# One expert table for both batches: layer 1's mixture of experts in 39 tiles instead of twice 23

## The chip, the core and the metric

The kernel runs on one core of a Trainium2 chip. Its time is measured on the device, in microseconds (us) for one execution; the kernel before takes 1811.49 us, the median of 19 runs that lie between 1807.17 and 1817.41 us. The engines are named as the profile names them: PE multiplies matrices (PEld loads its weights), DVE and ACT work element by element, POOL (GpSimd) issues the gathers and some element-wise work, and SP issues the plain transfers.

## What is computed

A model of four layers works on two batches of 1024 tokens with 128 features, all in float32. Each layer normalizes its input, computes an attention part `s` and a feed-forward part `g` from the same normalized input, and adds the product:

```python
xn = _layernorm(x, axis=-1)
s = _L1_attn_ref(xn, ...)
g = _silu(_L1_ffn_ref(xn, ...))
x = x + s * g
```

The feed-forward part of layer 1 is a mixture of experts. Eight experts, each a 128-to-512 product, a GELU and a 512-to-128 product; every token goes to the two of highest probability, whose results are added with these probabilities as weights:

```python
probs = jax.nn.softmax(jnp.einsum('bsd,ed->bse', x, Wr), axis=-1)
topv, topi = jax.lax.top_k(probs, K)                      # K = 2
h = jax.nn.gelu(jnp.einsum('bsd,dh->bsh', x, w1) + bb1, approximate=False)
y = jnp.einsum('bsh,hd->bsd', h, w2) + bb2
acc = acc + ce[..., None] * y                             # over the 8 experts
```

Nothing in it joins the two batches.

## The kernel before

The program is first recorded and then issued. Every call such as `C.mm(...)` or `nc.vector.tensor_add(...)` only notes an operation; products of one kind that follow each other are collected in one unit (`Record.note`, `Record.product`). A unit carries what it depends on. `Record.order` then reads a fixed order of all units from a packed string, `ORDER`, which was searched offline with a planner's costs, together with the place in memory of each buffer (`PLACES`). `Record.issue` emits the units in this order, so each engine's queue is fixed when the kernel is built, and every instruction of the profile carries the one line of `issue`, L584. The parts of the program are told apart by the names of their tiles.

The order interleaves freely: while one batch is in layer 1, the other may be in layer 0 or 2, as far as data allow. An instruction waits in its engine's queue until its inputs and its buffer are there, and everything behind it waits too.

Layer 1 has two parts.

- `l1_attn`, once for each batch: 64 steps of four `sim` products (scores, 32 rows deep), four exponentials on ACT (`e<-sim,own`, 128x512) and four `av` products that add up the weighted values. A finished sum is copied out by DVE (`asb<-av`).
- `l1_ffn`, once for each batch. It writes the normalized tokens to a table in memory (`xd`), takes the router's probabilities, ranks the experts of each token and counts the tokens of each expert (`rank`, `sel`, `before`, `place`). Each expert's tokens get whole tiles of 128 rows. For 2048 choices (1024 tokens, two experts each) and 8 experts there are at most (2048 + 8 * 127) // 128 = 23 tiles. 32 products (`fill`, 46 columns wide) put into a table which token stands in which row and with which weight. Then, for each tile, POOL gathers its 128 tokens (`xg<-xd,token`, 64 KB) and the weights of its expert (`we<-in_experts,expert`, 526 KB). Four `up` products, a bias on DVE, a GELU on ACT, and four `down` products follow; up to four tiles share one transposition, one scaling by the weight (`y<-down,weight`), and one write to a second table (`yd`). Last, POOL gathers the two results of each token back, 16 gathers of 128 rows each (`y<-yd,slots`), and DVE adds them (`g<-g,y`).

The layer's end (`step`) takes the SiLU of `g`, multiplies it by `s` and adds it to `x`; then the normalization of layer 2 (`ln_m`, `ln_sq`, `ln_v`, `ln_r`, `xn`) and the transposition `tr<-const,xn` of that batch can start. In layer 2, `l2_ffn` compares all tokens' router weights on DVE (`j<-wall,wtok`), and `l2_attn` runs the products `pk`, `pq`, `pg`.

The expert weights use the pool of 35 large buffers (`half`), the gathered tokens and the hidden values the pool of 21 buffers of 128x512 (`t512`), which also holds the exponentials of the attention. A gather is released when the buffer's former user has finished.

Of the kernel before, what the change touches and what calls it, by code (L numbers as in the profile page):

```python
# [19 lines left out]
I32 = mybir.dt.int32  # L20
# [5 lines left out]
P = 128  # L26
# [173 lines left out]
def _constants():  # L200
# [33 lines left out]
        "token": p + P * c[:, :8],  # L234
# [35 lines left out]
def pack_inputs(inputs):  # L270
# [38 lines left out]
    "c-nP&2VfLc_x+ytW@cx1Q%EI*gc^Dk5S1!H1O*F4P*4=%6G0IavCy(K!4Cv!is*;ZMN|}2iZmhg-g^rz1k#huwwd>TZ)SJ1!QX#LHd9`?@7{CIJ@0||XiL"  # L309
    "%ZXCXdr8|Xg0gHMv+rLh+fU7Uny6yB>{RM(AzF4Tr5;gZdL`$_y&2eej$InQhvxv=y0F()V*<Fx8o-5+bw_!)AeFops@KEDB;J|~q1XJc`_<}T|i#v~{^@"  # L310
    "C37INe=)Cgy^-Ec~3=2Os|63HwHJ)0vcQO2VSe&Zq;u{a4B}*-8yq`>!aivH-MQRSy+L6PVV>x6Q;iVH?E*MZV*1^NZzf;dOd}y*W&NXS+FJ~<@jqAStVx"
    "8*q0=ydJqG2ZGwkCyE~L$Z_XVMA+738mJTK!#Shqi5>KPM@HHzw#pkM2l=O{w(x*~J!{`1SGiCAEbe-zd^&4L7@o_eiE_?)sL|pSQYz2G+q4;I(8#wT6<&"
    "mGee(hc9{%3RZEse&%SNY5j>W~_^opQKp^4(<M*^R)hRAg5XV_&Lkm~yiko><|pPj%opks85|GtJI5<S&dboavB<SmdElhJBw@_QG~_!q%4j1w(u;@E~E="
    "3!U+^&7D(uFMoJ(pw(-AurcXrEbG_xfBlZoD?=x@?fw=XxHjOqZ})Uo{VLv@FEL6M4OM}3_`5c_C-aVkWkG$vWA8fYWYI5uc=V6q5m*avW1xM|;>B-%--@"
    "<!+upzr9i`6P{d1=ueC$3n8*n38xe@ZJ1S}ZQ=D4HD>BoVmCpW0XpKbi?*Tnm~`T&$X_SH>3QPtv427jA*?s9Ftpyu_W#%EKCip!K|327%yL)-mrFBHVO@"
    "+2uct$5Ua;IV_{F*}C$bMbbQoRkRzSGBECQ_3l-cC)b7wPtrxhr}w$OQC5?-a2sg-*K<-A=ps($l*Bi=B3hzcKGMXKdpZM6Nr;RN3@e1ko_{213iCxiLa>"
    "luUOGbfB!6qhhjrt(W@W^yMc%_9AEm5;-e)OS{CceB-c~WE5|A`ti$hF0kr^F{_%ohjQn8|uIDL^TKLEhJIBHZbrudN38^CPKvqQDsIR>y7%nRIlG?bIa("
    "&P*eKM~}o_QZM8uG#1IR*}HR29w@pX9ByKB{Dk%Y+<aJgQW9I|Wh2#Zf5Aw?;(b7HarCstBNh%XMgGo4gBc_Eo#trVD-;v?YB<SD!@5cRf}6xG58r2)_%H"
    "c=XAC{Y8){9G=KBt0v`wLgKd)|6Bekjv|hnh*EH@5<a%^k^PXicR_SfH1~`ztIpk_UR~N#QkI|i=2DWAbnj(J^3p%=k<`0Le44I`?y(xam~0iLR=iFsXA`"
    "Ud_cu6Sblc4BSOJ`G{*R)4iT6)o2wW-_Z(rMYQx2_^m;4k~ClL0OIq#-|o=J;oZ-Da<u%<uycYRgiREA|<6@{R2lAcpJ`$yBv52Y(nOYllnlo6tl0wrp8V"  # L320
    "Jx(|9Vm46U4b#)bneT!{UTKlUz{shJjt%%oD7|2soXpDkB+OJmE!&It6O$y0<09@zs~eH;fH+d+P?g+KcO&Icm<TP0#xBHdI7(e5k{GfKh+DBNd8UF163p"
    "WyD~fFYb|T6arX)*`>l{zA@?|EV@@-|=gGKJj#=}M>^1DV=Yti?W4fq4=B8npr2Tm3L)W<ZJ}V<A`S1sBKt7_~gnacX5{e}~0%Ysc+R0XWQH)*|NeI*3k%"
    "YMwnN^bXf~OA<O31y$K?Jj@hvU5rv9)FY^ry7yIkdFKdz&ul9;sAulp#^lq1VsUFQEy&n1(jHWg=<1#O$2TQKm#u=7K|8|J84xRxb}pKRgpt5T9R(F^}lU"
    "!G2ZDo*Uzi6JD=}gH}*C2nDwT_esprR6M4gh!ZX=KrD|_4Al$r0f!Q!7YTwQyn<+dNT?BmD!NV58S%$cM)IPIDCdSIINDlb`&&^a@%Zpi5b9DmFIVA&dqd"
    "TKMju@!@GDlgX6L=ixY;)M9UU>(%6Pr_HM9MuF9%X8tA4^{MtF71eSR2{4#<bH&?usE<-zTL{`2HqGNbweyisjFVq82HCF)<@(fO(ijbq0?_T~G&uYr|v*"
    "2lVp8RG_Z_FwU8_OvxGM?XVXM-_kFJm)n$rOx4ncMQc0e8K~1C#=o>eV;#46W5;n_-~A!{lyrUW9H(^wzu(R6>7z~DtysJ98lEJo)amzI-d7>513VDv{zF"
    "Y(>(Htf_CpXC@WLq@}o=Ux;S#Ca90(A%qYS3OyaA;otqQy;huNJ55X7FlxVCdp5(>*$V=;ASjUlRfVIokGFmWT1JzR(y(b-4>N9eS<B$VpF_Cm_eKD0(tg"
    "&CMts!FW`}wgY_Sxef|FZ{2?w(S0IvVTOM`HSTnsU1}R@FeYJEX7@N>y1Z?YWUq$=&o^+kBjDM4O&^<`0~9MM|YAq4iJKz2>$N9xlGhq|3>YM($P5N^pzn"
    "O>*N6$Y<+riTRbx{-wRhLQMHu;~Zn<5SE~N9QH!Kwn+M&zVJAs91f|s^9L^f^aq|TE-3E2K=MTMgjabAefM|5hSWQa@iUe9iX`1Zcee$Jjlqd{iE&p_jzL"
    "C<)opwElaZNw(Mn<myLR2mfs_X>EttKSMDPZsk+c#D^fER6e07epLaW{5mvvTI(r`bDv%Z6y7{$HKvr4<28u#{?G#pzr|Lmf19s%JLUjEG-jN=^&lL_vBR"  # L330
    "P-xhcN2~+4CC1a_b9abIDfqvCXUJMtX*lKe>{EcEDm^wNDt~!6pgcq&BK#D5xDDto#&#WGl@Hq2sZgRDh_E^pQ_ArY+BL~>GH`7kJQ5a@$0&6?z|p<USGM"
    "s*-4DqjIPM_->j95{D>p1Qfz0Ay@u6jaqR?}wTt+v!TD$Vw?278Lq_$jT?Q)8wd{7f`4RhC+GA|Y<vu+Ip~j6R*MXDGaN>JT{iE9gsjXaO(`$cj!;%FtE8"
    "p7C*WEFbzipm^xhXGvm5Sv*ebsZ+lar2LcrvNjrEsP7(-2YAYpr>K{buX=%8QRe+0%!jbny2HMYJ@5^W}M@qU8PWvSK;y7y9&#Z!GS27uc%lqwf7^O@Dn;"
    "PI8yO(PiuE{wpL8=fuVMzQK|<gU}SC3Stu@3Zj>PXWe|QHqahTrbfvab_&uuuG`YF{Uxj_cnRBkVqH6BdpeG!@9Icr4Z<;9I@<C+61a$9R8Rgxr!BBKA@?"
    "bA3}|*Tn-NPj@4YVgd%$0vN)qo={DC&Nxr#+xjo8z-+G5SeS7WxsJ$N2_+a}7my>8MWUVSz<MoY|hV#|z-^ZSrCa8?X<HEGxwf7^MnXt>W?b%?yb&g`9i@"
    "UHCNft^xZ|F7Oz)?`mRT=|c{f?a1@@j>11I%e)XQ8MV~+)V7zXQ9c=o{tSbyeTfPacq7K*L_)IR{9N(>5Ero9C>3YUi1ztT64=@R&8CcbwC3?PE>JyTxxR"
    "sR9Dc5i%pkw;t~ekZ&tf`j;wge*6sK7ozffUGrBgIuvWW)s+cz0UJyaA&KiSz%ckR8Ay?hQ&eh|}dl8zxS^r}mRlFX#x$RP(Wh>vsoJ(~}F8+CiA$HhyE4"
    "auT`TdnzM=|2yV+V&9jR59d!~!~J`Pp}{W7tmz-oo}c)JjFdQCxX|H?Pe@(x}Blv5Itzx`qEa2F^(+nK~b+)BP`?#}|D+Z{227H(0-Hd?-PuNPC<MU!5wM"
    "?RQ#9w`^>~*(fxseblZsaV?pkT`feiEzXCl7g7t_XS(CBqe)yPa=MZ4S`CuDWZYT%2K3$7E$;={yTaWS*!G_lj68a5=exV(v(rlub%haEQwcZk9Iw-PA4x"
    "rLE$uqv)9szJmLe)0myzB4K%F%84)VHvRqf8uEr${sNe3chha>LJjE1q5y5gn8x5p6H;<Nks67Tq@WhXazZso=2uKu-jG`Zgm17E|V4T{o`sl7O}I`zE#J"  # L340
    "sZ5_LCq7(CR!@x!d)2O;_#?%-*P}&+4_>+-dSzdd&3n^PK<SmZ+xXMqi&7K(Hj<AYBdFzIy`OkxarxtUjO+I8=me^2yeoJfibnm(SGiApZa4<XXmJ6k36L"
    "p&868M_{iL`{eF$UvSzS9(f$cR{$ZPYlcGC3YNvMZMZHvMC2qw!hF<+4>7A>-;zzmoYJI?uT}R(0*2b5=ScLccku|gN0lxlV4oV~P#%n3}VmJd4S?kgU89"
    "5}fwDR-6m6C|Dc(;@cDT};?Go3S8+qNS<s>aCl^qdnDz|n|l<LTJx<3EM<(-~8y7U8{hc{_U!CXNo>-?Pqg%P56h6wPaVq)(9%g{!D7eY<-(6i%=?oVw-c"
    "EY+3y+m2H^($^%8B=Wu4yABp)yNjMkJ?`uK#fO=2-PIx^%HrB>wiTfAZJ-8LzP=2NVulZ>ufEa-7#h*b5D-f^eCMGx#1Al{)-_A*QJAzIZTkI4dDYJ&?h*"
    "RhOf1V^TWvS~m~({FK<h)tAK`7Uq#cg!{XhTP#~xLdl1yOs+P**U{d$mX_7R8ULBf7)BX3@xyU1R$qiSy)`F2=y>?JqF97((D;yP^4ZXEFb3kk!%k3Ebgr"
    ">ob!T$_|WUpfT|BNj@D@h%QilE-4Npj8Cfi3TLshCG(v6t27iH`?61l^mT18eOJ1y8Nj-yq-#zi!tvTcrfx0kgmTWKd#Bu+}kD0(ffLCOx2Ucx2oM5iuEn"
    "uec4`WTej}SR~^<8U$1qlh8rX3A9ZNXAwT{eQ{+%e;tn^DD6qxIIQ7hyZl_!-OVpGU>N^yp+aKMcH$TzX=BN7ACMRtzPU2DAQqSs<$wYG9sCV1XOHB3a)v"
    "uO4c={}z`N`*BH3d0O^|n_b>9wYli03=8AKLEpVf%j~uarbTmW%6DUo&9UjN~&H6W6|#tJJun_|+8yt~T<VlKY>fO%9z^>YZsyPeZMF+0_Rdo6=;i;jVu@"
    "97=VN@83M(J40y?E4!pt*K~(=5e*rk7v}rfDD9hhmonQ(bk4|{S@XDly}kzjs~M-x9y3Fh9mtbExW0qt&3kcVde8m`@px}k`hY%AWvbR3xCSrAyrxoEHFe"
    "fBz$Z5T^39evWo7>(aecfI^Q?(?l*{#AS;`z)sRug4ujWy%4xb}2C}CD@d57~I_oR$jaKO%Y<9&Chp7h#I&RAK7M{WCP(}us{pP7H7!%slvoleKm+@yl&="  # L350
    "6^hQ;=C^PK6@S0-y5(R{o&i#V{6w9U3P2U>_kcN;reTc>Waya<8_XlNzRt^*o)WF^jn(ZwjS&l|HzSFXe&D4mo9&F-q~@lA2l!WR7vbW|NF*SM%u4H3!J}"
    "1s-!;n<iD+<IQR(XBM&t^(&7|Tp4rju$}w53eY@5zBr7=3idnBb-gx&#zL5o5ad0aN&iUGK%~1yIv$j^ZciY^0-zb`b-+FA_+kw{kwyxa$vli+h45XJ1+>"
    "hwIhgMb910Cz8@LkKKcHJg`j-US4i54hHy_0sa9@&DlD}T4>u|WlRtwd}~O*xXw93I{3wd#NHZI+hlSj~DOsqvi?>~VF6EsE4UpsH$N<-*uo{4cHI@U85a"
    "N+RhVwLZ5>jUtcZr+({7R9hUL1I;4)6~ek@Z_^7R)H0P)+Y?(7TAZf0*}>1S{<Gt2J1Q(wlA+s+m3G!mtxmSnk2F67IfmX#(vq-c@McPDD9m=Gu?qF{{6z"
    "<~r}lYhSws`ZUPn`}c0g_C(Gjr~PdN5by%pq=NFP0jC(!H0QTS_kkKoei*+XzSRe}b4$<4;gdz?NUIe>C$($ozVId>6NrD${dCfNN?WTKtE4R7IEUi^*vr"
    "z0AdZUz^O&x4#k*Ryio>4wyLruZ=%#$Yz!-%4H4w2aG1zSVI>(n2?xj&U9A$lYHWQ;oO~Lli7%;;3_?sYhP@XnyRoo0>jIzT5N%+snX(6^AzeGksjDZIm-"
    "@4@s_4c#o00nH|`kPm$SvYKMA^IQ)vI^8L!YSW|uY3lzP6=X;T7b{>l@_*ll*^`$4SJSZwol+M>;t(SbXsok>dk@$i*m&Q=yj(qy>#);o^l^lg6H)rb?<@"
    "H^xIP{oHP~2AcbDUharEeBDPk%<oUe4+~Gc~&P*PmQR?z;H*qL!*2RL?r{`S0FWeY|wT6E$H_wIZkO)Blc{J7MnVA88ljr^XRf1Kcl}`*w8EM%EqgcRJVX"
    "e*CEExO556KzW@?w^LknWz7BwgFe`lx*@juc)eIXb>`rkzfCM7Rj*HJ(PiemSvZ{wYwi5_(TKkjV;vC{6A;wHRj+Lx{)71+&AhPWY`wze;<VwZZ5T#|)%f"
    "(%=GwKcVP;RHts8M0m#}@(3Jm;mA>T(_X!KX&=Wlj@;n(@MaI=07KG3lK>C0+iSm!O@R-KW4o_sLAxa+eUdzVIRLz|Wh@(?%jOSs&86CjQL40Oce|12ycY"  # L360
    "}_JR7F(K^sCuF(?hZeUlU;v*cN8D2S+;|#<~N4K<t<qICf!SCe>ktyfp?b-S>XF%;k!IKOBF5c&aC{;fKTsKB|pAM*y?LvtU5LI6b@!-iT5Sl4b**W!QC<"
    "PVv4~_hH6vvzQ7}#gxRc*zU12T+RR0)<#FcCOeB@_P&{}(?2({xht}YPcj>}IybO-+`}h&G+|OlP{_=U3NE$|9zUi~KzX3kkICs>FT8CO6imTm8FiP>U76"
# [808 lines left out]
def l1_attn(C, w, xnT, b, out):  # L1171
# [157 lines left out]
    wT = C.arr("wT")  # L1329
    C.to_channels(wT, wt)  # L1330
    out["s"] = C.arr("s")
    C.project(out["s"], wT, w["wp"], w["bp"])


def l1_ffn(C, w, xn, xnT, b, out):

    nc = C.nc  # L1340
    E = 8
# [992 lines left out]
```

## Time and profile before

| what | value |
|---|---|
| median of 19 runs | 1811.49 us (1807.17 to 1817.41) |
| profiled execution, its own time | 1815.68 us |
| its span, first to last instruction | 1814.0 us |
| granted PE clock, mean | 0.958 |
| PE busy | 1649.6 us, 91% |
| DVE busy | 1206.6 us, 67% |
| ACT busy | 996.4 us, 55% |
| POOL busy | 552.3 us, 30% |
| gathers on POOL in layer 1 | 46 `we`, 46 `xg`, 32 `y` |

The profiled execution lies 4.19 us above the median, and its span 1.68 us below its own time. Busy time counts instructions that run, not waits; a group's `x` counts instructions, and one product in float32 is two matrix instructions.

### The profile page before, as it was taken

The numbers are of one execution on the slowest core, as the hardware profiler recorded it, in microseconds if no ns is written. First come the engines' busy times: TensorE is split into PE (matmuls) and PEld (weight loads), VectorE is DVE, ScalarE is ACT, GpSimd is POOL, SyncE is SP. The second block draws the span as 40 slices with busy tenths as digits, with TensorE's granted clock in tenths as the row PEclk, the third lists the DMA queues.
The fourth block names the chain that finished last, engine by engine and source line by source line (L and its number), as shares of the span: only waits on it lengthen the run. The fifth ranks groups of instructions, "written<-read, shape, count | busy, mean of one in ns | idle before, by whom it ended". The sixth has DMA issues, their size and how long they took to land.

```text
span 1814.0 us, 35482 instructions
## 1 busy us (share of the span) xinstructions
PE 1649.6 (91%) x14112; PEld 903.5 (50%) x14112; DVE 1206.6 (67%) x2371; ACT 996.4 (55%) x1775; POOL 552.3 (30%) x732
## 2 busy tenths in 40 slices
PE   7999998889699969699999999989999999999996
PEld 3464556543233823136746547743435665443374
DVE  5874895572211504333589999767988997967865
ACT  3322432249588559596465556566565565665632
POOL 1010012040511232411120165263723662873211
PEclk9998998889999979799999999999999999999998
DMA  3200010010411330313303023421003333101031
GB/s 113 32 14 2 2 34 14 2 59 24 140 38 20 118 103 20 102 17 108 116 22 102 26 67 91 137 75 61 19 5 100 98 87 90 38 28 49 24 99 45
DMA packets 96054, 106.23 MB, mean 59 GB/s; under 512 B 50224, under 2 KB 62512, under 8 KB 95760
## 3 DMA queue, kind: packets, MB, share of 16 engines
q1 hardware_dynamic: 86608, 74.11, 14.3%
q0 software_dynamic: 9280, 29.86, 5.5%
q8 instruction: 111, 1.82, 0.4%
q14 instruction: 55, 0.45, 0.1%
HBM read 87.24 MB, written 8.29 MB: 53 GB/s over the span
## 4 chain that ended last, share of the span: by engine, by line
PE 27%; DVE 18%; issue 6%; DMA 3%; ACT 3%; POOL 2%; SPq 1%; another core or an unknown queue 0%; DVEq 0%; ACTq 0%; POOLq 0%
PE sim L584 6%; DVE e L584 5%; PE num L584 4%; PE wo L584 2%; PE tr L584 2%; PE down L584 2%; DMA zb<-zd 2%; DVE qf L584 1%; DVE u L584 1%; SPq L584 1%; PE up L584 1%; PE g L584 1%; ACT e L584 1%; PE q L584 1%; PE qk L584 1%
## 5 line engine op out<-in xcount | busy, mean ns | idle before, releaser
L584 ACT ACTIVATE e<-sim,own 128x512 f32<-128x512 f32 x512 | 305.2, 704 | 90.6 <-remote 43.1
L584 ACT ACTIVATE e<-sim 128x512 f32<-128x512 f32 (+3 forms) x384 | 165.1, 499 | 94.7 <-DVE e L584 40.5
L584 PE MATMUL sim<-qT,k 32*128 32x512 f32 x1024 | 170.6, 682 | 43.4 <-DVE g L584 13.0
L584 DVE TENSOR_TENSOR e<-e 128x512 f32<-128x512 f32 (+3 forms) x320 | 171.3, 570 | 54.0 <-PE num L584 32.3
L584 PE MATMUL num<-e,v 128*64 128x64 f32 (+4 forms) x1280 | 166.7, 387 | 0.6 <-POOL e L584 0.4
L584 POOL TENSOR_SCALAR_AFFINE_SELECT e<-e 128x128 f32<-128x128 f32 x256 | 111.4, 466 | 152.6 <-ACT e L584 138.1
L584 PE MATMUL sim<-q,kT 64*128 64x512 f32 (+3 forms) x768 | 146.4, 510 | 7.1 <-ACT e L584 4.1
L584 PE MATMUL av<-e,va 128*32 128x512 f32 x1024 | 141.0, 641 | 6.2 <-ACT e L584 6.2
L584 PEld LDWEIGHTS sim<-qT,k 32*128 32x128 f32 x1024 | 53.2, 196 | 146.2 <-ACT e L584 86.1
L584 PEld LDWEIGHTS num<-e,v 128*64 128x64 f32 x1280 | 79.5, 138 | 86.3 <-issue 55.8
L584 POOL TENSOR_TENSOR sq<-qk,tab 128x256 f32<-128x256 f32 x128 | 100.7, 807 | 60.3 <-DVE ss L584 33.0
L584 PE MATMUL ph<-h,w_f 128*128 128x512 f32 x256 | 115.3, 601 | 1.1 <-DVE nn L584 0.7
L584 POOL DMA_INDIRECT we<-in_experts,expert x46 | 46.0, 999 | 205.9 <-DVE row L584 69.3
L584 PEld LDWEIGHTS sim<-q,kT 64*128 64x128 f32 x768 | 61.5, 185 | 88.2 <-ACT e L584 61.2
L584 DVE COPY asb<-av 128x512 f32<-128x512 f32 x16 | 11.1, 691 | 121.2 <-PE av L584 64.8
L584 POOL DMA_INDIRECT xg<-xd,token x46 | 45.0, 979 | 149.8 <-ACT e L584 85.6
L584 POOL TENSOR_TENSOR u<-u,sq 128x512 f32<-128x512 f32 x64 | 85.4, 1344 | 2.2
L584 ACT ACT_TABLE_LOAD x44 | 56.5, 1283 | 40.9 <-DVE h L584 7.8
L584 DVE SCALAR_TENSOR_TENSOR conv<-vT,w_a,conv 128x1024 f32<-128x1024 f32 x60 | 76.7, 1281 | 1.2
L584 PEld LDWEIGHTS ph<-h,w_f 128*128 128x128 f32 x256 | 47.9, 192 | 58.4 <-issue 54.3
L584 PEld LDWEIGHTS av<-e,va 128*32 128x32 f32 x1024 | 24.7, 112 | 95.9 <-issue 72.9
L584 ACT ACTIVATE e<-e 128x512 f32<-128x512 f32 x96 | 56.7, 626 | 27.7 <-DVE e L584 25.7
(545 smaller groups left out, 3424.9 us busy)
## 6 DMA issues: line engine op xcount, KB each, us to landing
zb<-zd SPq DMA_DIRECT2D x192, 128.0 KB
rb<-rd SPq DMA_DIRECT2D x64, 128.0 KB
w<-v SPq DMA_DIRECT2D x60, 128.0 KB
tab<-in_rotary SPq DMA_DIRECT2D x8, 512.0 KB
yd<-y SPq DMA_DIRECT2D x10, 256.0 KB
w_f<-in_f SPq DMA_DIRECT2D x4, 512.0 KB
w_l<-in_l SPq DMA_DIRECT2D x4, 512.0 KB
w_f<-in_f SPq DMA_DIRECT2D x4, 448.0 KB
```

The source lines that it names most:

```text
L584: tc.keep_in_program_order(f(*map(real, args), **{k: real(v) for k, v in kw.items()}))
```

## The change

`l1_ffn` is called once, after both batches' `l1_attn`, with the inputs of both. Both batches' tokens stand in one table `xd` of 2048 rows. The router, the ranking and the places are still made for each batch, with the second batch counting on from the first (`before`); the tiles are shared: (4096 + 8 * 127) // 128 = 39. The tables `rows`, `put` and `eq` are made for one batch and one of the two choices at a time, and the 32 `fill` products all add into one bank, now 78 columns wide. The results of both batches lie in one table `yd`, from which each batch gathers its own 32 pieces in two halves as before. The `step` of both batches comes after the call.

Products with at most 64 columns and a full 128x128 weight are collected in units of at most four, not 32. `ORDER` and `PLACES` are new: the whole program's order, all four layers, was searched anew.

```diff
-        "token": p + P * c[:, :8],
+        "token": p + P * c[:, :16],
...
-    def note(self, cost, op, args, kw, lag=SEEN, table=0, part=None):
+    def note(self, cost, op, args, kw, lag=SEEN, table=0, part=None, most=32):
...
-        if not (PE in cost and u and u.part == part and (u.batch, u.stage) == (self.batch, self.stage) and len(u.ops) < 32):
+        if not (PE in cost and u and u.part == part and (u.batch, u.stage) == (self.batch, self.stage) and len(u.ops) < most):
...
-        u = self.note({PE: 0.0}, op, args, kw, part=(tall, wide))
+        u = self.note({PE: 0.0}, op, args, kw, part=(tall, wide), most=4 if n <= 64 and tall * wide == P * P else 32)
...
-def l1_ffn(C, w, xn, xnT, b, out):
+def l1_ffn(C, w, xns, xnTs, outs):
...
-    E = 8
-    NTILE = (2 * L + E * (P - 1)) // P
+    E, NK = 8, 2
+    NTILE = (NK * NB * L + E * (P - 1)) // P
...
-    xd = C.memory("xd", [L, P])
-    nc.sync.dma_start(out=xd.rearrange("(t p) d -> p t d", p=P), in_=tiles(xn))
...
+    xd = C.memory("xd", [NB * L, P])
+    ranks, probs, sels, combs, befores = [], [], [], [], []
+    for b, (xn, xnT) in enumerate(zip(xns, xnTs)):
+        C.record.batch = b
+        nc.sync.dma_start(out=xd[b * L : (b + 1) * L].rearrange("(t p) d -> p t d", p=P), in_=tiles(xn))
...
+        before = C.t512("before")[:, : (TB + 1) * E].rearrange("p (t e) -> p t e", e=E)
+        if b:
+            nc.vector.tensor_copy(before[:, 0], befores[b - 1][:, TB])
+        else:
+            nc.gpsimd.memset(before[:, 0], 0.0)
...
+            for a in range(TB):
+                C.mm(
+                    pf[:, : 2 * NTILE], rows[:, cols(a)], put[:, a].rearrange("p s j -> p (s j)"),
+                    start=b == k == a == 0, stop=b == NB - 1 and k == NK - 1 and a == TB - 1,
+                )
...
+    for b in range(NB):
+        C.record.batch = b
+        acc, cT = C.arr("g"), C.arr("cT")
...
+        for k in range(NK):
+            y = C.arr(f"y{k}")
+            for t in range(TB):
+                gather(y[:, cols(t)], yd, slots[b][:, k * TB + t : k * TB + t + 1])
+            nc.vector.tensor_add(acc, acc, y)
+        outs[b]["g"] = acc
...
         for layer in range(4):
+            made = []
             for b in range(NB):
...
                     stage(l1_attn, weights("l1"), v[1], b, r)
-                    stage(l1_ffn, weights("l1"), *v, b, r)
+                    made.append((*v, r))
+                    continue
...
                 step(xb, r)
+            if made:
+                xns, xnTs, rs = zip(*made)
+                stage(l1_ffn, weights("l1"), xns, xnTs, rs)
+                for b in range(NB):
+                    C.record.batch = b
+                    step(x[b], rs[b])
```

In the new queues, as built, POOL has 39 `we`, 39 `xg` and 32 `y` gathers. Twelve `we` stand ahead of the first `xg`, and the rest of the 78 follow mixed; the `y` gathers of batch 0 come after the last `xg` and `we`. On PE, the last 44 `down` products (11 tiles) are followed by 32 `sim`, 36 `av` and 8 transposition products of batch 1's attention, and then by the eight transpositions `tr<-const,xn` with which batch 0 enters layer 2. Before, batch 0's `y` gathers and its `tr<-const,xn` stood among batch 1's attention, ahead of batch 1's expert tiles.

## The prediction

> **What bounds the kernel now.** I read the busy shares and the forty slices first, then the waits, then the windows and the timeline around the dips.
>
> ```profile
> PE 1649.6 (91%) x14112; PEld 903.5 (50%) x14112; DVE 1206.6 (67%) x2371; ACT 996.4 (55%) x1775; POOL 552.3 (30%) x732
> PE   7999998889699969699999999989999999999996
> DVE  5874895572211504333589999767988997967865
> PEclk9998998889999979799999999999999999999998
> ```
>
> PE is the bound: it stands still for 164.4 us of 1814.0 (1814.0 less 1649.6). The dips to 6 (slices of 45.35 us, from 454, 635 and 726 us) lie in layer 1, batch 1's attention, where DVE is nearly idle. The clock dips there too. So what the change does in layer 1 is worth PE time removed plus holes removed, less holes made. The waits name somebody who is not to blame:
>
> ```profile
> POOL y L584 <- DMA yd<-y: 45.9, 1, 45.9
> DVE asb L584 <- remote: 56.3, 2, 30.1
> DVE g L584 <- remote: 24.4, 1, 24.4
> ACT e L584 <- remote: 43.1, 10, 9.6
> ```
>
> The columns are total wait, times and longest. "Remote" is no engine of this core. The timeline shows what runs then: POOL issuing gathers back to back, one each 1.25 us (0.95 and 0.30 between), and PE standing.
>
> ```profile
> 667.98 0.95 POOL L584 DMA_INDIRECT y<-yd,slots  x1 [0.31 <-issue]
> 669.23 0.95 POOL L584 DMA_INDIRECT we<-in_experts,expert  x1 [0.30 <-issue]
> ...
> 643.78 1.14 PE L584 MATMUL sim<-qT,k 32*128 32x512 f32 x8
> 674.38 2.09 PE L584 MATMUL sim<-qT,k 32*128 32x512 f32 x8 [13.01 <-DVE g L584]
> ```
>
> The PE's hole of 13.01 us ends when the train of gathers does, and the eight matrix instructions behind it take 2.09 us against 1.14 ahead. Every such train can be priced as the PE's idle time in its window, the width less the busy time:
>
> ```profile
> core 0: us, PE busy (x) PEld busy (x) DVE busy (x) ACT busy (x) POOL busy (x), PEclk, DMA share, GB/s
> 465.00:503.00 38.00, 22.61 (x144) 6.02 (x136) 3.98 (x14) 17.88 (x30) 24.00 (x27) 0.83 0.54 177
> 590.00:618.00 28.00, 28.00 (x248) 25.64 (x247) 21.33 (x50) 16.63 (x26) 10.79 (x10) 1.00 0.41 124
> 646.00:675.00 29.00, 14.44 (x89) 5.47 (x91) 2.75 (x4) 11.25 (x19) 18.14 (x19) 0.69 0.39 118
> 730.00:761.00 31.00, 17.18 (x104) 3.95 (x100) 4.52 (x15) 14.16 (x25) 19.91 (x22) 0.76 0.48 149
> 866.00:1045.00 179.00, 169.28 (x916) 107.07 (x915) 156.47 (x308) 98.61 (x156) 29.30 (x31) 1.00 0.20 63
> ```
>
> Three long trains (27 gathers: 12 `we`, 15 `xg`; 19: batch 0's 16 `y`, 3 `we`; 21: 14 `xg`, 7 `we`) cost 15.4 + 14.6 + 13.8 = 43.8 us, 0.65 per gather. Four short ones (windows from 529, 571, 702 and 810 us, some 22 gathers) cost 1.45 + 2.87 + 1.75 + 3.26 = 9.3 us, 0.42 each. Batch 1's `y` train, among layer 2's products (895 to 921 us), costs 3.3. Spaced `we` gathers alone (590 to 618 us) cost nothing. Together 56.4 us.
>
> **The change part by part.** *A, PE work removed.* 46 tiles become 39. A tile is four `up` and four `down` products of two instructions each, and the chain of waits prices them:
>
> ```profile
> 848.12 11.61 PE up L584 x104
> 859.73 7.15 PE down L584 x64
> ```
>
> That is 0.112 us an instruction, 0.223 a product, 1.79 a tile: 7 x 1.79 = 12.5. Seven transpositions of `xg` at 0.15 (the transpositions of `asb` take 6.1 us for 40) are 1.0. The 32 `fill` products widen from 46 to 78 columns; they take 0.116 us an instruction at 46 (7.4 us for 64), products of 128 columns 0.112, so the width costs nothing. A = -13.5. The tiles' other work is priced at nothing: DVE has room beside PE (0 to 5 tenths in the slices from 408 to 861 us), and ACT's share of a tile is short.
>
> *B, the gather trains.* In the new POOL queue seven `we` and seven `xg` are gone. I grouped the rest by the PE work that frees their buffers: twelve `we` come early and spaced (nothing); 18 and then 23 (25 `xg`, 16 `we`) fall into the attention; some 25 among the expert products; batch 0's `y` train moves out of the attention (its price stands under C); batch 1's stays among layer 2's products. At the long trains' 0.65 the first 41 cost 26.7; at the short ones' 0.42 the 25 cost 10.5; batch 1's `y` 3.3. Sum 40.5, so B = -15.9. Ends: everything in attention at 0.42 and the 25 free, 20.5 (B = -35.9); all 66 at 0.65, 46.2 (B = -10.2). I keep 0.65 in the attention because three trains agree on it.
>
> The Trainium skill ("Trainium Architecture — The Big Picture", section "What this means for kernel authors") says that the engines' lanes into SBUF and the DMA ports can't contend. By it a train costs PE nothing of itself, B would be 0 and the sum +23. The 13.01 us hole, under a POOL that does nothing but issue gathers, speaks against taking it so far.
>
> *C, a new hole between layers 1 and 2.* This is the part that speaks against the change. Before, batch 0's way into layer 2 (last `yd` store, sixteen `y` gathers, sum, SiLU, normalization, transposition) lies under batch 1's attention, and batch 1's under batch 0's layer 2:
>
> ```profile
> 889.58 1.16 DVE L584 TENSOR_TENSOR y<-down,weight 128x384 f32<-128x384 f32 x2
> 895.23 0.94 POOL L584 DMA_INDIRECT y<-yd,slots  x1 [45.91 <-DMA yd<-y]
> 917.02 0.94 POOL L584 DMA_INDIRECT y<-yd,slots  x1 [0.30 <-issue]
> 919.57 1.23 DVE L584 TENSOR_TENSOR g<-g,y 128x1024 f32<-128x1024 f32 x1 [2.61 <-DMA y<-yd,slots]
> 942.81 1.04 PE L584 MATMUL tr<-const,xn 128*128 128x128 f32 x8
> ```
>
> After, batch 0 needs all 39 tiles before its first `y` gather, and batch 1's experts are done by then. By the rows: 5.65 us from the last `y` product to the first gather, 15 x 1.25 = 18.8 to the last, 2.55 to the sum, 1.23 for it, 14.45 from SiLU (696.85) to transposition (711.30), as batch 0 did it, and one load of ACT's function table, 1.28. Together 44; batch 1's row, from 889.58 to 942.81, took 53.2 among layer 2's work. What covers it is what the new PE queue puts between the last `down` and `tr<-const,xn`: 32 `sim` and 36 `av` products, eight steps of attention. A step is four exponentials on ACT, one behind the other 2.42 us, a little more than its PE work. 8 x 2.42 = 19.4. So C = +24.6 (44 - 19.4); ends +23 (the same with the table load hidden) and +34 (53.2 - 19.4).
>
> The skill's page "TensorE: Matmul & The Clock Gate" (section "What's actually happening") says that PE falls to half clock once it has idled some 3.4 us, and needs as long a stretch of work to recover; by it this hole costs an estimated 1.7 us more. The row of 2.09 against 1.14 us shows the half clock after a long hole.
>
> *D, batch 0's comparisons on DVE.* Layer 2's `j<-wall,wtok` (mean 0.747 us, 46 in all, and 16 of 0.35) is some 20 us a batch. Batch 0's ran from 727 us, under batch 1's attention; now it stands at the start of layer 2, where DVE is busy 156.5 of 179 us. Room is 22.5, less its bad placing; between 0 and 20 I take +8 (no gain: DVE stood idle where they were).
>
> *F, late weights.* After, the expert products of all 39 tiles run nearly in one piece, and the last 14 tiles need their 526 KB each within it. At the 149 to 177 GB/s of the train windows a tile's weights take 3.0 to 3.5 us against 1.79 of PE, but the queue runs ahead by the buffers. Weights can't be earlier than needed to any gain; 0 to 10, I take +4.
>
> *The units of four and the new order elsewhere.* Layers 0, 2 and 3 keep their sequence nearly as it was on all queues; nothing taken, 10 us either way. ACT loads as many tables as before.
>
> Sum: -13.5 - 15.9 + 24.6 + 8 + 4 = +7.2. The profiled execution's span of 1814.0 becomes 1821.2; its own time, 1.68 above, 1822.9; that execution lay 4.19 above the median, so the median becomes 1818.7.
>
> **The rivals.** *Faster.* Trains that stand among expert products cost nothing (28.00 busy of 28.00 from 590 to 618 us, though only `we`), those in the attention 0.535, the mean of both prices, and the weights arrive in time: 41 x 0.535 + 3.3 = 25.2, B = -31.2, F = 0, sum -12.1, time 1799.4. Against it stand the expert window from 810 us, which lost 3.26 of 10, and three trains at 0.65.
>
> *Much slower (the other end of my own side).* The way into layer 2 takes batch 1's 53.2 us, the comparisons lie bare, the weights are late: -13.5 - 10.2 + 34 + 20 + 10 = +40.3, time 1851.8. For it: DVE's nines in layer 2. Against: in the hole POOL and DVE have little else, whereas batch 1's train shared both with layer 2.
>
> *No net change, or the change is undone elsewhere.* Gains and losses cancel, B near -23, or B as taken with D at 0 (sum -0.8); or the new order loses or wins some 7 us in layers 0 and 3. Time 1811.5.
>
> Faster becomes the outcome once the trains cost under 33 us in all: with F at nothing the sum is +19 and B.
>
> **How the numbers follow.** A measurement of this kernel can tell 0.2%, 3.6 us. My forecast has 0.40 (slower, 1815 to 1835), the faster rival 0.37, the cancelling one 0.11, the much slower one 0.12. Faster 0.37, same 0.11, slower 0.52. The range must take in the faster rival with some of B's lower end and most of the way to the much slower one: 1790 to 1846; outside it lie half of that rival and a little of B's low end. The predicted time is the forecast's, 1818.7.
>
> **What would show it.** In the profile after: PE's matrix instructions fewer by 119 (seven tiles of 17); one hole of PE of about 25 us between the last `down` and `tr<-const,xn`, with sixteen `y` gathers in it, and a POOL wait for `yd<-y`; the "remote" waits of DVE gone or halved; windows around the `xg` trains with 0.4 to 0.65 us of idle PE per gather; layer 2 longer by about 8 us with `j` in it. C is wrong if that hole is under 15 us, B if the trains' idle sum is outside 20 to 46, and D if layer 2's DVE hides `j`. The whole is wrong if layer 0 or 3 differs by more than 10 us.

## The result, and the profile after

| | before | after |
|---|---|---|
| median | 1811.0 us (46 runs, 1805.26 to 1818.99) | 1835.68 us (7 runs, 1830.22 to 1839.49) |
| profiled execution, its own time | 1815.68 us | 1835.11 us |
| its span | 1814.0 us | 1833.4 us |

The ratio is 1.0135, 95% interval 1.0119 to 1.0151. The changed kernel is 24.7 us slower by the medians; the forecast said 7.2. The two profiles lie only 19.4 us apart, since the one of before was taken 4.7 us above its median.

The busy shares and slices of the kernel after:

```profile
PE 1658.7 (90%) x13991; PEld 907.3 (49%) x13991; DVE 1195.9 (65%) x2332; ACT 997.9 (54%) x1779; POOL 539.4 (29%) x716
PE   7999998979999787985799989999999999899996
DVE  6965984663223120232799999777798997967765
PEclk9998999879998898997899999999999999999998
```

PE has 121 matrix instructions fewer and is busy 9.1 us longer, and idle 10.3 us more. The expert tiles do take 9.2 us less of PE (their `up`, `down` and `xg` transpositions), but the same 1024 `sim` instructions of the attention take 177.2 us instead of 162.9, and most of that lies in the 80 of them that now stand behind the last `down`. The slices from 596 and 688 us (7 tenths) have trains of gathers in them; the deepest dip (5 tenths, from 825 us) lies between the layers, and DVE's nines begin two slices later. The timeline around it, first DVE and POOL, then PE:

```profile
823.34 0.56 DVE L583 TENSOR_TENSOR y<-down,weight 128x384 f32<-128x384 f32 x1 [1.99 <-PE down L583]
827.04 0.95 POOL L583 DMA_INDIRECT y<-yd,slots  x1 [31.86 <-issue]
...
845.77 0.94 POOL L583 DMA_INDIRECT y<-yd,slots  x1 [0.30 <-issue]
```

```profile
840.03 1.70 PE L583 MATMUL sim<-qT,k 32*128 32x512 f32 x2 [3.92 <-ACT e L583]
850.61 2.07 PE L583 MATMUL sim<-qT,k 32*128 32x512 f32 x2 [8.88 <-DVE asb L583]
...
866.10 3.64 PE L583 MATMUL av<-e,va 128*32 128x512 f32 x16 [4.90 <-ACT e L583]
...
871.45 1.92 PE L583 MATMUL av<-e,va 128*32 128x512 f32 x16
873.31 1.09 PE L583 MATMUL tr<-const,xn 128*128 128x128 f32 x8
...
899.14 3.78 PE L583 MATMUL pk<-w_l,xnT 128*128 128x512 f32 x4 [6.50 <-DVE asb L583]
```

The hole between the layers is there: sixteen `y` gathers, 50 us from the last scaled expert result (`y<-down,weight`) to `tr<-const,xn`, and in it eight steps of attention with idle PE before and between them. Behind a hole of 4.90 us sixteen `av` instructions take 3.64 us; sixteen more, from 871 us, take 1.92.

The windows (PE idle is the width less the first number) of the trains, of the way into layer 2, and of layer 2:

```profile
core 0: us, PE busy (x) PEld busy (x) DVE busy (x) ACT busy (x) POOL busy (x), PEclk, DMA share, GB/s
598.00:633.00 35.00, 24.06 (x161) 6.53 (x153) 2.73 (x4) 20.69 (x35) 14.17 (x15) 0.76 0.23 69
676.00:706.00 30.00, 12.80 (x48) 2.23 (x42) 0.00 (x0) 8.89 (x15) 16.33 (x18) 0.62 0.60 179
823.20:873.30 50.10, 30.95 (x145) 9.78 (x144) 12.20 (x16) 22.52 (x33) 21.71 (x22) 0.73 0.26 87
873.30:1079.00 205.70, 186.08 (x904) 103.57 (x900) 190.56 (x387) 113.88 (x183) 39.88 (x41) 0.98 0.14 42
```

In layer 2 DVE is busy 190.56 of 205.70 us. The same window of the kernel before, from its last `down` to its last `pg`, was shorter by more than 37 us:

```profile
890.00:1058.00 168.00, 158.67 (x796) 93.04 (x796) 155.07 (x309) 96.12 (x157) 37.70 (x40) 1.00 0.19 59
```

So the span was cut at five marks, taken from the start times of the named products in the trace. The second pair of columns is from both kernels run again (next section).

| stretch | first pair: before, after | difference | second pair: before, after | difference |
|---|---|---|---|---|
| start to the first `sim` of layer 1 | 392.7, 378.8 | -13.9 | 389.5, 376.0 | -13.5 |
| to the 64th step of attention | 193.3, 166.6 | -26.7 | 165.1, 165.5 | +0.4 |
| to the last `down` | 303.7, 277.6 | -26.1 | 263.9, 229.0 | -34.9 |
| to the last `pg` of layer 2 | 168.3, 255.9 | +87.6 | 170.3, 244.4 | +74.1 |
| to the end of the span | 756.0, 754.5 | -1.5 | 755.6, 756.3 | +0.7 |

Ten steps of attention moved from the third row into the fourth, 24.2 us at 2.42 each. Without them the fourth row still grows by 63.4 and 49.9 us. That is where the loss is. Not all of it is lost time: before, batch 0's `tr<-const,xn`, `row`, `wtok`, `pk`, `pq` and `pg` took 10.0 us of PE ahead of the last `down` (9.6 in the second pair), and after, none; that work left the third row and came into the fourth. The comparisons did the same on DVE: 21.3 us of `j` stood ahead of the last `down` before and none after, while the fourth row's went from 21.1 to 42.3 us.

### The profile page after: what moved, and what is told of

Same layout as the page of the kernel before. It is cut to its first block, busy times and chain, and to the rows that moved or that the text cites. A ratio compares the mean times of both kernels' runs of the same rounds, so it can differ in the third digit from the quotient of the medians.

```text
span 1833.4 us, 35151 instructions
## 1 busy us (share of the span) xinstructions
PE 1658.7 (90%) x13991; PEld 907.3 (49%) x13991; DVE 1195.9 (65%) x2332; ACT 997.9 (54%) x1779; POOL 539.4 (29%) x716
## 4 chain that ended last, share of the span: by engine, by line
PE 53%; DVE 26%; issue 8%; another core or an unknown queue 5%; ACT 4%; POOL 2%; DMA 1%; SPq 1%; DVEq 0%; ACTq 0%; POOLq 0%
PE sim L583 12%; PE av L583 6%; DVE e L583 4%; PE num L583 4%; PE tr L583 4%; PE ph L583 3%; DVE u L583 3%; PE down L583 3%; PE wo L583 2%; PE up L583 2%; ACT e L583 2%; DVE j L583 2%; DVE qf L583 1%; PE z L583 1%
## 5 line engine op out<-in xcount | busy, mean ns | idle before, releaser
L583 PE MATMUL sim<-qT,k 32*128 32x512 f32 x1024 | 184.7, 685 | 46.5 <-ACT e L583 24.1
L583 PE MATMUL num<-e,v 128*64 128x64 f32 (+4 forms) x1280 | 165.4, 384 | 1.4 <-POOL e L583 0.9
L583 PEld LDWEIGHTS sim<-qT,k 32*128 32x128 f32 x1024 | 62.9, 196 | 153.7 <-ACT e L583 105.2
L583 PEld LDWEIGHTS av<-e,va 128*32 128x32 f32 x1024 | 24.7, 111 | 107.8 <-issue 83.8
L583 POOL DMA_INDIRECT xg<-xd,token x39 | 37.2, 954 | 138.0 <-ACT e L583 126.9
L583 PE MATMUL qk<-w_f,shifted 128*128 128x512 f32 x128 | 63.1, 611 | 5.6 <-DVE u L583 1.9
```

The lines of the kernel that those rows point to most:

```text
L583: tc.keep_in_program_order(f(*map(real, args), **{k: real(v) for k, v in kw.items()}))
```

## The experiments

A time is given as the median, and as the ratio to the kernel before in the same session (on the same chip, close in time) with its 95% interval, because the sessions differ: the kernel before has a median near 1748 us in some and near 1811 us in others. I call these the 1748 and the 1811 setting; the result above is of the 1811 setting. Kernels with the same order of layer 0 reached layer 1 between 373.8 and 383.7 us in the 1748 setting, so effects of a few us are read from the length of a stretch, and not from the whole time: layer 2 of the changed kernel, from the transposition of `xn` to the last `pg`, took 204.2 to 206.5 us in the nine runs in which nothing in it was edited.

### Both kernels again

> The changed kernel a second time, to see which differences of the two profiles repeat. Both theories: 1830 to 1840 us. Theory A (the way of batch 0 into layer 2 costs what is missing): the stretch from the last `down` product to the end of the `asb` copies in layer 2 again takes about 80 us for some 33 us of PE work. Theory B (products run slower all over): PE's busy time is again about 9 us above the kernel before in several stretches, not in this one alone.

> The kernel before a second time, with its profile, to lay stage beside stage on one chip: the trains in the attention held up PE in the first profiles (43.8 us) and not at all in the second profile of the changed kernel. Theory C1 (how hard a train holds up PE belongs to the chip, and the change costs about 25 us on either because its other terms are larger than I took them): on a chip with a median near 1748 the three train windows lose under 6 us of PE, near 1811 some 40. Theory C2 (trains always hold up the kernel before): over 30 us on either.

Both came out in the 1748 setting, on two chips. After: 1773.26 us, ratio 1.015 (1.0122 to 1.0178). Before: 1748.09 us, 0.9986 (0.9934 to 1.0037). The same trains of the kernel before, there:

```profile
463.00:500.00 37.00, 37.00 (x288) 13.23 (x284) 6.66 (x19) 35.94 (x62) 24.03 (x27) 1.00 0.58 182
604.00:640.00 36.00, 35.73 (x287) 14.66 (x285) 12.07 (x17) 33.36 (x58) 18.77 (x19) 1.00 0.40 116
680.00:708.00 28.00, 26.32 (x195) 8.33 (x191) 12.50 (x32) 26.17 (x45) 19.68 (x22) 1.00 0.57 165
```

In either setting these are 25, 19 and 21 gathers at the same pace, with POOL as busy, and PE loses 1.95 us instead of 43.8. So the program does not fix how hard a train holds up PE. What does is not shown: theory C1 put it down to the chip and its numbers came true, but the record has chip number 10 in both settings, with the kernel before at 1748.28 us and, eighteen minutes later, at 1809.76 us. In the 1748 setting the rule of the Trainium skill that I weighed against my row ("Trainium Architecture — The Big Picture", "What this means for kernel authors") agrees with the measurement; in the 1811 setting it does not. The change costs 24.7 us in the one setting and 25.5 in the other, though the trains, its largest gain in the forecast, are worth nothing in the second.

### The comparisons alone

```diff
-            j[:, : v.shape[1]], v, wc, None, op, ALU.add, accum_out=acc[:, t : t + 1]
+            j[:, : min(8, v.shape[1]) if b == 0 else v.shape[1]], v[:, :8] if b == 0 else v, wc, None, op, ...
```

> The changed kernel with batch 0's 23 comparisons `j` of up to 1024 columns cut to 8 columns each, so that batch 0's ranks in layer 2 are of too few tokens. It takes some 14 us of VectorE's work out of the start of layer 2. Theory D2 (VectorE is the bound there, and the comparisons cost what they last): 11 to 18 us less than the changed kernel. The prediction's D (most of it lies in gaps of VectorE): 4 to 8 us less. With the copy `asb` moved first there was no gain, which speaks for D2.

> The same cut in the kernel before, where batch 0's comparisons run under batch 1's attention. Theory D2: within 3 us of the kernel before, since VectorE idles there. Rival (those instructions cost wherever they stand): 8 us less or more.

The changed kernel: 1824.31 us, 1.0062 (1.0041 to 1.0084), against 1.0135: some 13 us less by the ratios, 10 by the medians. The kernel before: 1.0000 (0.9981 to 1.0019). So the comparisons were hidden before, and no longer wholly are. But the stretch tells less than the ratio: layer 2 shrinks from 205.6 to 200.2 us, by 5.4, while DVE lost 12.8 us of work:

```profile
873.00:1073.00 200.00, 185.44 (x898) 102.68 (x896) 177.80 (x387) 113.97 (x183) 38.16 (x41) 0.98 0.15 43
```

So the cut itself is worth 5.4 us of layer 2, within D of the prediction, and does not explain the 30 that layer 2 grew: more than half of the comparisons' time found cover there. The other part of the 10 to 13 us is not in this profile, which is of the slowest of the ten executions (1830.55 us).

In the first trace of the changed kernel `pk` waited 6.50 us for `asb`, which stood behind comparisons. It was moved ahead of the last of them:

```diff
 VectorE: ... j x17, ...
-j x9, asb, j ...
+asb, j x9, j ...
```

> The changed kernel with one thing moved in VectorE's order: the copy `asb` of batch 1's last attention group stands ahead of the last nine or so of the comparisons `j` that it stood behind. Theory D (batch 0's comparisons hold up PE through that copy: holes of 5 to 6.5 us before `pk`): 4 to 7 us less than the changed kernel. Rival (VectorE is the bound there whatever its order): 0 to 2 us less.

1775.70 us, 1.0145 (1.0106 to 1.0184), against 1.0150: nothing. Layer 2 took 207.7 us instead of 205.4. PE no longer waited for `asb`; a few us later the transposition of that `asb` waited 6.38 us for `k`, which stood behind the comparisons in its turn. Reordering moved the wait and left DVE's work, as the rival said.

### Batch 0's start of layer 2

```diff
 order of the kernel before, on every engine:
-... row, wall, wtok, j x31, pk, pq, pg ... (batch 0, layer 2) ... last down
+... last down, then tr<-const,xn, row, wall, wtok, j x31, pk, pq, pg ... (batch 0, layer 2)
```

> The kernel before (23 tiles a batch, its own order), in which only batch 0's start of layer 2 is put off: the transpositions of its `xn` and the 66 units of layer 2 that stood ahead of batch 1's last `down` (31 `j`, `row`, `wall`, the first `pk`, `pq`, `pg` with their VectorE and ScalarE work) follow directly behind that `down` on every engine. No tile, no gather and no wait between the layers is changed. Theory G (the changed kernel loses mainly because batch 0's start of layer 2 no longer lies under batch 1's attention and experts): 18 to 32 us more than the kernel before, and the stretch from the last `down` to the last `pg` grows from 170 to 190 to 202 us. Rival (D as I took it: some 8 us of the comparisons come to lie bare, the rest is free): 4 to 10 us more.

> The same with batch 0's 23 comparisons cut to 8 columns (ranks of too few tokens), some 14 us less of VectorE's work. If the comparisons are the price: within 6 us of the kernel before. If the whole start of layer 2 is: 5 to 8 us below the run with the start put off alone, as in the changed kernel, where the cut shortened layer 2 by 5.4 us.

1848.05 us, 1.0212 (1.0177 to 1.0247): 38.3 us more, with no other change; more than either theory gave. From the last `down` to the last `pg` it takes 212.2 us instead of 168.3. With the comparisons cut: 1837.31 us, 1.0142 (1.011 to 1.0173), and 200.1 us. The windows of the two, and PE's hole in the first:

```profile
877.00:1089.20 212.20, 173.74 (x832) 99.38 (x831) 187.09 (x390) 99.81 (x163) 37.61 (x40) 0.92 0.16 48
```

```profile
881.00:1081.10 200.10, 175.11 (x832) 99.60 (x831) 174.29 (x390) 100.06 (x163) 37.52 (x40) 0.95 0.17 51
```

```profile
908.38 2.07 PE L584 MATMUL pq<-xnT,w_l 128*128 128x512 f32 x2 [23.89 <-DVE k L584]
```

DVE has 31.7 us more to do in this stretch than before (187.09 less 155.37 for 889.70 to 1058.00), and PE waits 23.89 us because `k` stands behind all the comparisons on DVE. My order of it is cruder than the one of the changed kernel, whose layer 2 grew by 30 and not by 44, and where the longest such wait was 6.50 us. So the run shows the mechanism and its direction, not its size in the changed kernel: take batch 0's start of layer 2 out from under batch 1's attention and experts, with nothing else changed, and the kernel before becomes slower than the changed one. With the comparisons cut, 31.8 of the 43.9 us remain. The cut takes 13 of the 21 us of comparisons that were moved, and 12.1 us of time; at that price all of them would be worth some 20 us (an estimate), so it is not `j` alone.

### The wait between the layers

```diff
+                if op == "indirect_dma_start" and u.batch == 0 and kw["in_"].name.startswith("yd"):
+                    tc.keep_in_program_order(tc.nc.sync.dma_start(out=real(kw["out"]), in_=real(kw["in_"])[:P]))
+                    continue
```

> The changed kernel, with batch 0's sixteen `y` gathers replaced by sixteen plain transfers of the same size by SyncE (which read the same 128 rows of `yd`, so batch 0's sums are of other rows). Theory A (gathers in a train hold up both the way of batch 0 and the attention that was to cover it): the train's 18.8 us go, the attention steps keep 2.42 us each, the stretch behind the last `down` falls from 80 to 45 to 55 us; 25 to 38 us less than the changed kernel, 1798 to 1811. Theory B (the loss lies in the expert products and late weights): 5 to 15 us less, 1821 to 1831.

> Batch 0's `y` by plain transfers once more, in the same hour as the other two. On a chip where the trains don't hold up PE (median of the kernel before near 1748): 2 to 4 us less than the changed kernel, as measured. On one where they do (near 1811): 10 to 18 us less, since the 12.8 us of idle PE under that train go as well.

1770.76 us, 1.0133 (1.0104 to 1.0163), and 1769.44 us, 1.0139 (1.0085 to 1.0192): 2.5 and 3.8 us less, both in the 1748 setting. From the last `down` to the transposition of `xn` it takes 33.9 us instead of 39.0. The way got shorter by 5 us and not by 18.8; the SiLU stands behind exponentials in ScalarE's queue, and they were not done earlier. Theory A fell with that in this setting; what the train costs in the other one was not tried.

Then the wait itself was taken away:

```diff
-            nc.vector.tensor_add(acc, acc, y)
+            nc.vector.tensor_add(acc, acc, acc if b == 0 else y)
 order: g, sg, x, ln_m, xn, ln_sq, ln_v, ln_r, xn of batch 0 stand among the last expert products
```

> The changed kernel without the wait between the layers: batch 0's sum leaves out the gathered `y` (its gathers still run), and sum, SiLU and normalization of batch 0 stand among the last expert products in their queues. Theory C (the way of batch 0 through `yd` costs PE 21 to 31 us, what its eight steps of attention don't cover): 18 to 31 us less than the changed kernel, so 0.985 to 1.004 of the kernel before. Rival (the attention behind the last `down` is bound by ScalarE anyway): 0 to 8 us less, 1.009 or more.

> The same with batch 0's comparisons cut to 8 columns as well. If waiting (C) and comparisons (D) are the whole loss: 31 to 45 us less than the changed kernel, 0.976 to 0.997 of the kernel before, which then shows what seven tiles less are worth. Rival (the two losses hide each other, since both hold up the start of layer 2): no more than 4 us below the run with the wait alone taken away.

1787.68 us, 1.0247 (1.0194 to 1.03), slower than with the wait; and with the comparisons cut 1780.24 us, 1.0178 (1.0115 to 1.0242), with layer 2 at 199.5 us instead of 205.4. Two things show why. The step made a hole of its own: on POOL `ln_r` waited for DVE with the gathers of weights queued behind it, and PE stood.

```profile
760.64 0.24 POOL L583 TENSOR_SCALAR ln_r<-ln_v 128x8 f32<-128x8 f32 x1 [19.39 <-DVE ln_v L583]
```

```profile
765.20 2.04 PE L583 MATMUL up<-xT,we 128*128 128x128 f32 x8 [11.97 <-issue]
```

And behind the last `down` the same eight steps, with nothing of batch 0 to wait for, still took 31.3 us, not 19.4. So of the 39.0 us only 7.7 were the wait. The rest is attention behind a break, at a mean clock of 0.84 in that window. The two edits together don't show what seven tiles are worth; that question was not answered this way.

> The changed kernel, with the ten units of `sim` products behind the last `down` issued twice each (same values): 40 products, 80 matrix instructions more, 10 us at full clock, 20 at half. Theory A (the stretch is bound by the way of batch 0 and by ACT, and PE's longer busy time there is room): 0 to 4 us more than the changed kernel, 1835 to 1840. Theory B' (PE at half clock is itself the bound there): 10 to 20 us more, 1845 to 1856.

1777.18 us, 1.0168 (1.0133 to 1.0204): 3.9 us more, 2.2 of them in the stretch to the transposition (41.15 instead of 38.96). PE was busy there for 37.6 us instead of 26.5, so most of the doubled work found room: PE is not the bound in that stretch.

```diff
 PE: ... down x16,
-down x16, down x12, sim x4 ...
+sim x4, down x16, down x12 ...
```

> The changed kernel with the first unit of `sim` products behind the experts moved ahead of the last two units of `down` products, so that ScalarE has four exponentials to do while PE does those. Theory C2 (the eight steps cover less than 19.4 us because the attention starts again from an empty queue: ScalarE waits 5.3 us for its first products): the first exponentials start some 5 us earlier, and 2 to 5 us less than the changed kernel. Rival (batch 0's way sets the end of the stretch, so that earlier steps only wait earlier): within 1.5 us of it.

1780.44 us, 1.0171 (1.0135 to 1.0208), no gain to be seen: 40.4 us to the transposition instead of 39.0. An earlier start of one step is not the cure.

```diff
 VectorE: ... asb,
-z, z, g, g ...
+g, g, z, z ...
 ScalarE: -e x4, sg   +sg, e x4
```

> As the run with `asb` first, and besides the sum `g` of batch 0 stands ahead of two reciprocals `z` on VectorE, and the SiLU `sg` ahead of four exponentials on ScalarE. Theory A (the way of batch 0 is the bound behind the last `down`): 2 to 6 us less than with `asb` first alone. Rival (ScalarE's exponentials are the bound and only change places): within 2 us of it, either way.

1782.94 us, 1.0180 (1.0143 to 1.0217). The interval still holds the 1.0150 of the changed kernel, but the stretch to the transposition is longer, 42.3 us. SiLU ahead of the exponentials did not help batch 0.

### What PE work costs among experts and in the attention

```diff
-            for op, args, kw in u.ops:
+            for op, args, kw in u.ops * (2 if u.n in [...] else 1):
```

> The changed kernel with the `up` products of every third tile issued twice (13 tiles, 52 products, same values). Term A of the prediction (0.223 us a product, all of it on the path): 11.6 us more than the changed kernel. Rival (the expert products wait for weights and for their hidden values, so that PE has room there): 0 to 5 us more, and then seven tiles less were worth under half of the 12.5 us that I took.

> The changed kernel with ten units of `sim` products of batch 0's attention, spread over its first 64 steps, issued twice (same values): 40 products, some 10.5 us of PE work, beside exponentials that come one each 0.605 us. Theory F (a step of attention lasts what four exponentials last, 2.42 us, so PE work beside it is free as long as it fits): 0 to 3 us more than the changed kernel, 1.014 to 1.017 of the kernel before. Rival (PE is the bound there, being over 90% busy): 9 to 12 us more, 1.019 to 1.022.

Doubled `up`: 1785.22 us, 1.0196 (1.0158 to 1.0234); the stretch from the 64th step to the last `down` grows from 229.0 to 240.2 us, 11.2 for 52 products, 0.215 each. Term A was sized rightly for this setting. Doubled `sim`: 1786.57 us, 1.0229 (1.0201 to 1.0257); the first 64 steps take 172.0 us instead of 165.4, 6.6 us more, and PE is busy there for 169.1 us instead of 162.1. So the doubled products added 7.0 us of PE work, and not the 10.5 expected, and nearly all of it shows: theory F falls, and PE work beside the attention in mid-stream is nearly full price.

### Spaced gathers, and layer 0 alone

```diff
+            if u.n in [...]:  # behind 44 of the gathers
+                tc.keep_in_program_order(tc.nc.gpsimd.tensor_tensor(s, s, s, ALU.pow))
```

> The kernel before, with a GpSimd power of 128x8 ones on a spare tile (about 1.7 us) behind each of 45 gathers: the first 15 `xg` of batch 0, batch 0's 16 `y`, and 13 `xg` of batch 1's long train; nothing left out. Theory A1 (gathers back to back hold up PE, spaced ones do not): most of the 43.8 us of idle PE in the three long trains goes, 20 to 40 us less, 1771 to 1791. Theory A2 (each gather has its price, spaced or not): within 4 us of 1811, and the holes are spread. Rival: the spaced `xg` come late to the expert products, 5 to 20 us more.

1784.23 us, 1.0207 (1.0165 to 1.025). It fell in the 1748 setting, where trains cost next to nothing, so it can't tell A1 from A2. It shows another price of spacing: the sum `g` waits 24.31 us for batch 0's spaced `y` gathers, with `asb` behind it on VectorE, and PE waits for that.

```profile
670.98 7.06 PE L586 MATMUL fill<-put,rows 128*128 128x46 f32 x32 [23.09 <-DVE asb L586]
```

> The kernel before, with layer 0 alone in the units of four and in the order that the changed kernel has there (each place of a layer 0 unit in the old order gets the next unit of layer 0 in the new one; layers 1 to 3 keep theirs; some buffers are other ones). Theory E (the new order of layer 0 gains some time, which hides part of the loss in layers 1 and 2): 3 to 10 us less than the kernel before. Rival (batch 1 enters layer 1 earlier only because work was put off): within 2 us.

1816.98 us, 1.0032 (1.0012 to 1.0052): no gain, and the first `sim` of layer 1 at 388.0 us, against 389.4 in the kernel before with the comparisons cut, in the same session. The 13.5 us by which the changed kernel reaches layer 1 earlier are not layer 0's order by itself; in the second pair PE has 9.4 us less to do by then, which comes later. What the rest is stays open.

## Why the prediction was wrong

The direction was right and the size was not: +24.7 us measured, +7.2 forecast (1835.7 against 1818.7, inside the range of 1790 to 1846). The 10.0 us of PE work that only changed its row is taken out of the fourth row here and given back to the third. By its own steps, with the first pair of profiles:

| step | forecast | measured | from |
|---|---|---|---|
| A, seven tiles | -13.5 | -9.2 and -13.8 | busy time of `up`, `down` and the `xg` transpositions, first and second pair |
| B and F, trains and late weights | -11.9 | -5.1 | second and third row, less A, the ten steps and the 10.0 us moved |
| C, hole between the layers | +24.6 | +30.9 | 50.3 less 8 x 2.42 |
| D, layer 2 | +8 | +22.5 | 205.6 from the transposition of `xn` to the last `pg`, less 168.3 before, less two steps of 2.42 and the 10.0 us moved |
| layer 0 and the border | 0 | -13.9 | first row |
| layer 3 | 0 | -1.5 | last row |

With A at -13.5, which the second row presumes, these make +19.4, as the profiles lie apart; the medians add the 5.3 us by which the two profiled executions stood nearer to each other.

**The step that failed is D.** I asked which work the change moves into layer 2, found the comparisons, and let 8 us of their 20 come to lie bare. For the comparisons alone that was about right: 12.8 us less of them gave back 5.4 us of layer 2, which makes some 9 for the 21 that moved (an estimate). But they are only part of what moves. DVE does 35 us more in that stretch (190.56 less 155.07), since batch 0's whole start of layer 2, which lay under batch 1's attention and experts, now stands behind the last expert. Layer 2 grew by 22.5 us net in the first pair and by 20.7 in the second; my upper end for D, 20, left both out. The run with that start put off in the kernel before shows the direction by itself: +38.3 us, in a cruder order. How the 13 us or so beside the comparisons divide among the rest of that start no run of the changed kernel shows.

**A term at nothing hid part of it.** I took nothing for the new order elsewhere and called the whole wrong if layer 0 or 3 differed by more than 10 us. The changed kernel reached layer 1 13.9 us earlier, which is over that bound if the border is counted with layer 0; only 3.5 us of it are `fill` products that moved behind the mark, and the rest stays open. Without the other 10.4 us the loss would have been near 35 us. That the total stayed inside the range is in part luck.

**C was in its bounds on the first pair, for a reason I had not given.** I let the attention cover the wait at 2.42 us a step. In the profile the eight steps ran with 19 us of idle PE, under the `y` train and at a clock of 0.73; in the 1748 setting the same reckoning gives 19.6 (39.0 less 19.4), below my lower end of 23, and without any wait the steps took 31.3 us there. Cover has to be priced as it runs there, behind a break, and not as it runs in mid-stream. The Trainium skill's page "TensorE: Matmul & The Clock Gate" (section "What's actually happening") names the half clock behind idle time; the row of 3.64 against 1.92 us agrees. My estimate of 1.7 us was for one hole, and there were several: the 64 `sim` and 72 `av` instructions between the layers took 28.9 us of PE, where their mean price in the kernel before gives 19.6. How much of that is the clock was not separated.

**B was right in one setting and near zero in the other.** The first long train has 25 gathers and not 27 as I counted, so the price was 0.67 us a gather. In the changed kernel the trains fell where I had put them: 18 and 23 gathers in the attention with 28.1 us of idle PE, 25 among the experts with 8.6 (755 to 803 us), batch 1's `y` with 2.0 (910 to 934 us), 38.8 in all against 40.5. By these windows B is -17.6, and some 12 us were lost elsewhere in those two rows: A fell short by 4.3, the `fill` products brought 3.5, and late weights may be the rest. In the 1748 setting the price before was 0.03 us a gather. The total came out nearly the same there; that the second and third row gained 34.5 us instead of 52.8 was mostly made up by a hole and a layer 2 that cost 13.5 us less.

The faster rival fell: trains among the experts were not free in the 1811 setting, and C and D outweighed them. The much slower one named the right place for D, DVE's nines in layer 2, but it too counted the comparisons alone. No run beat the kernel before. The shared table and the newly searched order came together; beyond three small moves, no other order of the changed kernel was tried, so that a better one might lose less.

## What to carry to other kernels

When a change merges two chains into one step, list everything that used to run under the second chain, on every engine, and price it bare: what is lost is the overlap, not the step. Net out the work that only moves from one stretch to another before calling a longer stretch a loss. Price cover in the state in which it will run, and read a result by stretches between fixed marks, which repeat within two or three us where the starts of whole runs scatter by ten.

## What was not expected of the hardware

The same program ran at two levels that lie 3.5% apart (medians of 1748 and 1811 us), nearly all of it in layer 1: 429 against 497 us from the first `sim` to the last `down` of the kernel before. At the slower level PE stands while POOL issues gathers back to back, 43.8 us under 65 of them; at the faster one the same gathers at the same pace cost it 1.95 us. Each session kept to one level, and one chip number stands beside both. What makes the difference no run here shows.
